# Smaller closing steps, earlier addresses and an earlier check in a graph layer with a mixture of experts

## The chip, the cores and the metric

The kernel runs on one core of one Trainium2 chip. The metric is the time of one execution in microseconds (us) on the device. A core has five engines, each with its own program that it works through in order: TensorE (PE in the profile, its weight loads PEld), VectorE (DVE), ScalarE (ACT), GpSimd (POOL) and SyncE (SP). SyncE only issues transfers here; ScalarE and GpSimd issue some too. "SPq" and "ACTq" are these engines' instruction queues.

## The reference

6250 nodes with 256 features go through a graph layer and then through a mixture of 8 experts, each node to the two experts with the highest scores.

```python
deg = jnp.maximum(jax.ops.segment_sum(jnp.ones(dst.shape), dst, num_segments=6250), 1.0)
x = x + gnn(_layernorm(x), deg ** -0.5, W, b, src, dst)   # 106250 edges: (h @ W.T + b) * norm, summed by dst, * norm
h = _layernorm(x)
gate_scores = h @ Wg.T + bg                               # (6250, 8)
topk_scores, topk_idx = jax.lax.top_k(gate_scores, 2)
topk_probs = jax.nn.softmax(topk_scores)
for e in range(8):
    y = jax.nn.relu(h @ W1[e].T + b1[e]) @ W2[e].T + b2[e]   # 256 -> 1024 -> 256
    out = out + combine[:, e:e + 1] * y                     # combine holds the two probabilities
return x + out
```

All of it is float32.

## The kernel before

**Stream.** The nodes form 49 tiles of 128. The edges, sorted by destination, form 831 chunks of 128. A planner written in Python places the work in *slots*: slot s (L961 to L979) issues one indirect gather of 128 source rows on GpSimd (`gather`, L459), a mask on VectorE, the matmul that adds up chunk s on TensorE (`add_up`, L470), the *tasks* that are due in that slot, and as many pieces of expert work as a *credit* allows (`next_piece`, L938). The credit gains 1025 ns less the known work in each slot; `PIECES` (L57) says what a piece costs. Before slot 140, credit that is left is spent on filling matmuls (L978). As soon as all edges of a tile have been added up, its nodes go through normalisation, scores, choice of experts and sorting in stages of fixed slots, and are sent to queues in DRAM, one for each expert (`send`, L714).

**Steps.** Expert work goes in 61 steps: 52 with a slot of their own (`STREAM`, L38) and nine behind the stream (`TAIL`, L45). `choose` (L728) takes, on VectorE, the expert with most rows waiting, and up to n of its rows, n being the size of the step; it also notes in `at`, for every node, where its result will stand. SyncE loads the weights w1 (L775, 1028 KB) and w2 (L788, 1152 KB) and the rows (`xT`, L783). `up` (L808) has 8 pieces of four matmuls, each followed by a ReLU on ScalarE into `hid`. `down` (L820) has four pieces of four matmuls for each half of 128 rows; a slot behind the fourth, `leave` (L834) adds the bias on VectorE (y, L838) and SyncE writes y to `fyq` (L840). There are two output tiles `py`, so a half can start when the y of the half before last is done. From L928 to L936: up pieces of one step and down pieces of the step before it take turns.

**Behind the stream** (L997 to L1027) each slot s issues due tasks, at most one choice, one load of w2 and one of w1 and rows, one piece, and work of *reading back*: `DONE` (L71) lists after which step how many tiles are finished. When a listed step has been done for six slots and nothing is queued, `results` (L902) makes the addresses `rowat` of its tiles on VectorE; then GpSimd gathers the two results of each tile, one a slot (`read_back`, L907, three slots in four), into one of 12 buffers `yb`; eight slots later, or when more than ten wait, `take` (L988) adds them to the node rows on VectorE (`add_in`, L917). Every fourth tile a store of four tiles goes out from GpSimd (L994, L924).

**The end.** When the last gather of tiles 44 to 47 has been added, L1031 to L1051 make the addresses of tile 48, check that no row came later than its tile's bound (ten operations on VectorE and a matmul with one column, whose result `g.bad` decides at L1506 whether a slow second path runs), gather tile 48, and store the rest.

The order on each engine is the order in which this Python code issues (`manual_schedule`); waits are put in where data or buffers demand them.

Of the kernel before, what the change touches and what calls it, by code (L numbers as in the profile page):

```python
# [7 lines left out]
F32 = mybir.dt.float32  # L8
# [11 lines left out]
P = 128  # L20
N = 6250
NT = 49
# [22 lines left out]
TAIL = (256, 256, 256, 256, 256, 256, 128, 128, 128)  # L45
ROWS_OF = [n for s, n in STREAM] + list(TAIL)
USUAL = len(ROWS_OF)
START = [P + sum(ROWS_OF[:step]) for step in range(USUAL + 1)]

# [7 lines left out]
PIECES = {FT: (915, 870), P: (600, 870)}  # L57
# [91 lines left out]
def in_order(ctx: ExitStack, tc: tile.TileContext, g: Shared):  # L149
# [670 lines left out]
    def down(step, i, s):  # L820
        f = steps[step]
        a = i // 4
        if i % 4 == 0:
            f["py"] = psp.tile([P, D], F32, name="py")
        for b in (2 * (i % 4), 2 * (i % 4) + 1):
            nc.tensor.matmul(f["py"], f["hid"][:, b, a * P:(a + 1) * P], f["w2"][:, b * D:(b + 1) * D],  # L826
                             start=(b == 0), stop=(b == HB - 1))
        if i % 4 == 3:
            plan_at(s + 1, leave, step, a, f["py"], f["w2"])
        if i == 4 * ROWS_OF[step] // P - 1:  # L830
            del steps[step]


    def leave(step, a, py, w2):  # L834

        nonlocal gone
        y = work.tile([P, D], F32, name="y", bufs=4)
        nc.vector.tensor_add(y, py, w2[:, HB * D:])  # L838
        r0 = START[step] + a * P
        w = nc.sync.dma_start(yq[r0:r0 + P, :], y)  # L840
        free_order(w, reads, "results are written once, and read once written")
        writes.append((step, w))
        if a == ROWS_OF[step] // P - 1:
            gone += 1


# [91 lines left out]
    def next_piece(s):  # L938

        nonlocal curu, curd, done, upped, was  # L940
        was = next_kind(s)
        if was == "up":
            up(upped, curu)
            curu += 1
            if curu == HB:
                upped, curu = upped + 1, 0
        if was == "down":
            down(done, curd, s)
            curd += 1
            if curd == 4 * ROWS_OF[done] // P:  # L950
                done, curd = done + 1, 0
        return was

    with tc.manual_schedule():
        with rowp as rowpool:
# [5 lines left out]
            for s in range(NC):  # L961
# [8 lines left out]
                while credit > 0:  # L970
                    of = upped, done
                    kind = next_piece(s)
                    if not kind:
                        break
                    credit -= PIECES[ROWS_OF[of[kind == "down"]]][kind == "down"]
# [4 lines left out]
        with tc.tile_pool(name="ftail", bufs=2) as pool:  # L980
# [3 lines left out]
            got = asked = allowed = stored = 0  # L984
            latest = 0
            since = {}

            def take():  # L988
# [4 lines left out]
                if got == 2 * stored + 11:  # L993
                    store(stored, stored + 4, nc.gpsimd)  # L994
                    stored += 4

            while done < USUAL or tasks or len(plan) > 1 or asked < 2 * allowed or pend:  # L997
                for fn, args in tasks.pop(s, []):
                    fn(*args)
                if s > all_sent and s > max(STREAM)[0] + 6:  # L1000
                    if chosen < min(USUAL, upped + 4):
                        run(choose(chosen))
                        chosen += 1
                    if loaded2 < min(loaded1, gone + 3):
# [10 lines left out]
                if len(plan) > 1 and done > plan[0][0] and s >= since.get(plan[0][0], 0) + 6 \  # L1015
                        and asked == 2 * allowed:
                    step, t1 = plan.pop(0)
                    results(allowed, t1, float(START[step + 1]))
                    allowed = t1
                    latest = step  # L1020
                if asked < 2 * allowed and s % (4 if s > all_sent else 2):
                    pend.append((s, read_back(pool, rowat, asked // 2, asked % 2, latest)))
                    asked += 1
# [4 lines left out]

            results(allowed, NT, float(START[USUAL]))  # L1031
            late = work.tile([P, NT, 2], F32, name="late", bufs=1)
            missed = work.tile([P, 2], F32, name="missed")
            nc.vector.tensor_tensor(late, at, bounds, op=OP.is_ge)
            nc.vector.tensor_reduce(missed[:, 0:1], late, op=OP.add, axis=mybir.AxisListType.XY)
            nc.vector.tensor_reduce(missed[:, 1:2], most, op=OP.max, axis=mybir.AxisListType.X)
            nc.vector.tensor_scalar(missed[:, 1:2], missed[:, 1:2], float(SLOTS), None, op0=OP.is_gt)
            nc.vector.tensor_add(missed[:, 0:1], missed[:, 0:1], missed[:, 1:2])
            nc.vector.tensor_add(missed[:, 0:1], missed[:, 0:1], g.outside)
            ones = work.tile([P, 1], F32, name="ones")  # L1040
            nc.vector.memset(ones, 1.0)
            pm = psp.tile([1, 1], F32, name="pt", bufs=1)
            nc.tensor.matmul(pm, missed[:, 0:1], ones, start=True, stop=True)
            nc.vector.tensor_scalar(g.bad, pm, 1.0, None, op0=OP.min)
# [506 lines left out]
```

## Time and profile before

| | us |
|---|---|
| median of 9 runs | 1305.92 (1304.93 to 1308.49) |
| the profiled execution | 1304.85 |
| its span, first to last instruction | 1303.1 |
| gathers of edges on GpSimd, first and last start | 70.7, 1114.8 |
| TensorE's longest late gap, before step 52's first piece | 6.57, to 1169.22 |
| last down piece of step 60 ends on TensorE | 1281.08 |
| last addition ends on VectorE | 1296.34 |
| TensorE, VectorE, ScalarE, GpSimd busy | 1173.7, 979.5, 405.1, 907.9 |

The page gives busy shares, 40 slices of the span with the busy share of each engine in tenths, the chain of work that ended last, and groups of instructions. A timeline row reads: start, duration, engine, line, operation, tiles, count, and in brackets how long the engine had been idle before it and what ended that. In groups of matmuls the durations overlap, so starts are what counts.

### The profile page before, as it was taken

What the parts mean: (1) busy time and instruction counts of PE and PEld (TensorE: products, weight loads), DVE (VectorE), ACT (ScalarE), POOL (GpSimd) and SP (SyncE); (2) the same over time, 40 slices, a digit from 0 to 9 for tenths busy, and PEclk for the clock granted to TensorE, in tenths of its full rate; (3) what the DMA queues carried; (4) which work ended last, traced back from release to release, by engine and by line L of the source; (5) the groups of instructions that cost most, each with busy time, mean ns of one, the idle gap of its engine ahead of it and who ended that gap; (6) DMA issues with size and microseconds to landing.
All of it is one profiled execution on the core that took longest, in us unless ns stands there. A gap on an engine that the chain in (4) does not pass through costs nothing.

```text
span 1303.1 us, 24787 instructions
## 1 busy us (share of the span) xinstructions
PE 1173.7 (90%) x6562; PEld 914.1 (70%) x6562; DVE 979.5 (75%) x5472; ACT 405.1 (31%) x949; POOL 907.9 (70%) x976
## 2 busy tenths in 40 slices
PE   5368789799999899999999889899999999979993
PEld 5336567377777677777777667677777777758882
DVE  8924686767888878888888788887977785895532
ACT  3713233133333233333333233323232333222220
POOL 2167777777777777777777777777777777557733
PEclk9999989899999999999999999999999999989997
DMA  7463597878787887888888787878888887889983
GB/s 250 156 195 106 173 319 206 278 217 292 250 267 258 260 294 254 267 292 258 266 263 277 245 267 232 282 236 309 275 291 275 289 290 255 284 293 406 332 298 100
DMA packets 160927, 337.38 MB, mean 259 GB/s; under 512 B 26900, under 2 KB 106344, under 8 KB 145160
## 3 DMA queue, kind: packets, MB, share of 16 engines
q1 hardware_dynamic: 114348, 207.57, 45.6%
q0 software_dynamic: 46176, 127.59, 32.5%
q8 instruction: 54, 0.88, 0.3%
q14 instruction: 97, 0.79, 0.2%
q10 hardware_dynamic: 252, 0.53, 0.1%
HBM read 280.44 MB, written 55.16 MB: 258 GB/s over the span
## 4 chain that ended last, share of the span: by engine, by line
PE 59%; DMA 22%; DVE 10%; issue 3%; POOL 3%; ACT 1%; SPq 1%; POOLq 0%; ACTq 0%; DVEq 0%
PE ph L816 22%; PE py L826 19%; DMA rows<-ftable,src 16%; PE ps L475 10%; DMA yb<-fyq,rowat 3%; PE pt L568 3%; PE ps L978 2%; POOL yb L909 1%; PE px L700 1%; DMA xT<-fhq 1%; POOL rows L461 1%; PE ph L518 1%; ACT hf L364 1%; DMA fhq<-ordered 1%; PE count L295 1%
## 5 line engine op out<-in xcount | busy, mean ns | idle before, releaser
L461 POOL DMA_INDIRECT rows<-ftable,src x831 | 792.2, 953 | 274.7 <-issue 103.3
L816 PE MATMUL ph<-xT,w 128*128 128x256 f32 (+1 forms) x1952 | 474.8, 370 | 10.9 <-DMA xT<-fhq 8.3
L826 PE MATMUL py<-w,hid 128*128 128x256 f32 x1760 | 450.5, 381 | 0.1
L816 PEld LDWEIGHTS ph<-xT,w 128*128 128x128 f32 x1952 | 351.4, 191 | 115.5 <-issue 27.8
L818 ACT ACTIVATE hid<-ph,w 128x256 f32<-128x256 f32 (+1 forms) x488 | 220.3, 452 | 576.6 <-PE ph L816 468.7
L826 PEld LDWEIGHTS py<-w,hid 128*128 128x128 f32 x1760 | 329.3, 190 | 73.8 <-issue 3.4
L475 PE MATMUL ps<-rows,mask 128*128 128x512 f16 x831 | 312.4, 382 | 63.0 <-DMA rows<-ftable,src 33.3
L468 DVE TENSOR_SCALAR mask<-col_b,rel 128x128 f16<-128x128 bf16 x831 | 202.4, 270 | 8.5 <-PE ps L475 6.4
L909 POOL DMA_INDIRECT yb<-fyq,rowat x98 | 94.9, 969 | 62.6 <-issue 20.1
L475 PEld LDWEIGHTS <-mask 128*128 128x128 f16 x831 | 82.2, 100 | 56.0 <-issue 21.7
L575 DVE SCALAR_TENSOR_TENSOR xr<-pt,norm,xr 128x256 f32<-128x256 f32 x49 | 23.7, 484 | 92.5 <-PE pt L568 92.4
L838 DVE TENSOR_TENSOR y<-py,w 128x256 f32<-128x256 f32 x110 | 46.1, 419 | 62.4 <-PE py L826 62.1
L535 DVE SCALAR_TENSOR_TENSOR rolled<-rolled,keep,ps 128x256 f32<-128x256 f32 x149 | 70.5, 473 | 23.2 <-PE ps L475 23.2
L550 ACT ACTIVATE whole<-rolled 32x256 f32<-32x256 f32 (+2 forms) x156 | 63.8, 409 | 59.7 <-DVE rolled L538 57.4
L917 DVE SCALAR_TENSOR_TENSOR xr<-yb,prob,xr 128x256 f32<-128x256 f32 x98 | 46.1, 481 | 36.9 <-DMA yb<-fyq,rowat 36.2
L538 DVE TENSOR_TENSOR rolled<-ps,rolled 128x256 f32<-128x256 f32 x150 | 63.6, 424 | 5.1
L568 PE MATMUL pt<-gw,uT 128*128 128x264 f32 x196 | 51.9, 387 | 0.0
L639 ACT ACTIVATE h2s<-h 128x256 f16<-128x256 f32 x49 | 20.3, 414 | 91.8 <-DVE h L630 91.7
L978 PE MATMUL ps<-nothing 128*128 128x512 f16 x162 | 48.1, 415 | 0.0
L568 PEld LDWEIGHTS pt<-gw,uT 128*128 128x128 f32 x196 | 37.4, 191 | 12.7 <-issue 2.0
L295 PE MATMUL count<-oh,ol 128*16 128x8 bf16 (+2 forms) x898 | 28.8, 175 | 15.6 <-DVE oh L281 13.3
L597 DVE TENSOR_SCALAR rs<-ry,rv 128x1 f32<-128x1 f32 x147 | 39.7, 270 | 1.9
(187 smaller groups left out, 1133.5 us busy)
## 6 DMA issues: line engine op xcount, KB each, us to landing
w<-in_W SPq DMA_DIRECT2D x61, 1152.0 KB
w<-in_W SPq DMA_DIRECT2D x61, 1028.0 KB
fhq<-ordered SPq DMA_DIRECT2D x392, 64.0 KB
fyq<-y SPq DMA_DIRECT2D x110, 128.0 KB
rows<-ftable,src POOLq DMA_INDIRECT x831
xT<-fhq SPq DMA_DIRECT2D x49, 256.0 KB
out<-xr POOLq DMA_DIRECT2D x11, 512.0 KB
xr<-in_x SPq DMA_DIRECT2D x6, 896.0 KB
```

The source lines that it names most:

```text
L461: nc.gpsimd.indirect_dma_start(out=rows[c], out_offset=None, in_=table[:, :], in_offset=bass.IndirectOffsetOnAxis(ap=g.src[:, c:c + 1], ax ...
L468: nc.vector.tensor_scalar(masks[c], g.col_b[:, r:r + P], g.rel[:, c:c + 1], None, op0=OP.is_equal)
L475: nc.tensor.matmul(sums[w], masks.pop(c), rows.pop(c), start=(c == chunks[0]), stop=(c == chunks[-1]))
L535: nc.vector.scalar_tensor_tensor(new, rolled, keeps[kept[w]], ps[:, 0:D], op0=OP.mult, op1=OP.add)
L538: nc.vector.tensor_add(new, ps[:, D:2 * D], new)
L550: nc.scalar.activation(whole[t][p0:p1, :], new[p0:p1, :], AF.Copy)
L568: nc.tensor.matmul(pl, uT[:, k, :], gw[:, k, :], start=(k == 0), stop=(k == 1))
L816: nc.tensor.matmul(ph[:, :n], w1[:, k * H + b * P:k * H + (b + 1) * P], f["xT"][:, :n, k], start=(k == 0), stop=(k == 1))
L818: nc.scalar.activation(f["hid"][:, b, :n], ph[:, :n], AF.Relu, bias=w1[:, 2 * H + b:2 * H + b + 1])
L826: nc.tensor.matmul(f["py"], f["hid"][:, b, a * P:(a + 1) * P], f["w2"][:, b * D:(b + 1) * D], start=(b == 0), stop=(b == HB - 1))
L909: r = nc.gpsimd.indirect_dma_start(out=yb, out_offset=None, in_=yq[0:START[upto + 1], :], in_offset=bass.IndirectOffsetOnAxis(ap=where[:, ...
L978: nc.tensor.matmul(sums[WINDOW[s]], nothing[:, 0:P], nothing, start=False, stop=False)
```

## The change

The steps behind the stream get smaller, from 1920 rows in all to 1632, and need no longer be multiples of 128; `down` and `leave` work on what rows there are (m). In the planner an up piece costs `29 * rows // 8` ns, at least 300. When all steps have been issued, addresses are made in the next slot, whatever is still queued, and a gather goes out in every slot; tile 48 goes through the same loop, and stores issued then leave from ScalarE and SyncE. The check becomes a task in parts (`verdict`) that starts four slots behind the choice of the last step.

```diff
-TAIL = (256, 256, 256, 256, 256, 256, 128, 128, 128)
+TAIL = (256, 256, 224, 208, 192, 176, 128, 128, 64)
+HALVES = [-(-n // P) for n in ROWS_OF]
-PIECES = {FT: (915, 870), P: (600, 870)}
+DOWN = 870
...
+        m = min(P, ROWS_OF[step] - a * P)
         for b in (2 * (i % 4), 2 * (i % 4) + 1):
-            nc.tensor.matmul(f["py"], f["hid"][:, b, a * P:(a + 1) * P], f["w2"][:, b * D:(b + 1) * D],
+            nc.tensor.matmul(f["py"][:m], f["hid"][:, b, a * P:a * P + m], f["w2"][:, b * D:(b + 1) * D],
...
-        nc.vector.tensor_add(y, py, w2[:, HB * D:])
+        m = min(P, ROWS_OF[step] - a * P)
+        nc.vector.tensor_add(y[:m], py[:m], w2[:m, HB * D:])
-        w = nc.sync.dma_start(yq[r0:r0 + P, :], y)
+        w = nc.sync.dma_start(yq[r0:r0 + m, :], y[:m])
...
+    def verdict():
+        late = work.tile([P, NT, 2], F32, name="late", bufs=1)
+        missed = work.tile([P, 2], F32, name="missed")
+        nc.vector.tensor_tensor(late, at, bounds, op=OP.is_ge)
+        nc.vector.tensor_reduce(missed[:, 0:1], late, op=OP.add, axis=mybir.AxisListType.XY)
+        yield
+        nc.vector.tensor_reduce(missed[:, 1:2], most, op=OP.max, axis=mybir.AxisListType.X)
+        nc.vector.tensor_scalar(missed[:, 1:2], missed[:, 1:2], float(SLOTS), None, op0=OP.is_gt)
+        yield
+        nc.vector.tensor_add(missed[:, 0:1], missed[:, 0:1], missed[:, 1:2])
+        nc.vector.tensor_add(missed[:, 0:1], missed[:, 0:1], g.outside)
+        ones = work.tile([P, 1], F32, name="ones")
+        nc.vector.memset(ones, 1.0)
+        yield
+        yield
+        pm = psp.tile([1, 1], F32, name="pt", bufs=1)
+        nc.tensor.matmul(pm, missed[:, 0:1], ones, start=True, stop=True)
+        yield
+        yield
+        nc.vector.tensor_scalar(g.bad, pm, 1.0, None, op0=OP.min)
...
-                    credit -= PIECES[ROWS_OF[of[kind == "down"]]][kind == "down"]
+                    credit -= DOWN if kind == "down" else max(300, 29 * ROWS_OF[of[0]] // 8)
...
                 if got == 2 * stored + 11:
-                    store(stored, stored + 4, nc.gpsimd)
+                    store(stored, stored + 4, nc.scalar if gone == USUAL else nc.gpsimd)
                     stored += 4
+                elif got == 2 * NT - 2:
+                    store(stored, NT - 1, nc.sync)
+                elif got == 2 * NT:
+                    store(NT - 1, NT)
...
                         chosen += 1
+                        if chosen == USUAL:
+                            in_parts(s + 4, verdict)
...
-                if len(plan) > 1 and done > plan[0][0] and s >= since.get(plan[0][0], 0) + 6 \
-                        and asked == 2 * allowed:
+                if plan and done > plan[0][0] and (done == USUAL or s >= since.get(plan[0][0], 0) + 6 and not queue):
                     step, t1 = plan.pop(0)
                     results(allowed, t1, float(START[step + 1]))
+                    queue += [(t, j, step) for t in range(allowed, t1) for j in range(2)]
                     allowed = t1
-                if asked < 2 * allowed and s % (4 if s > all_sent else 2):
-                    pend.append((s, read_back(pool, rowat, asked // 2, asked % 2, latest)))
-                    asked += 1
+                if queue and (done == USUAL or s % (4 if s > all_sent else 2)):
+                    t, j, step = queue.pop(0)
+                    pend.append((s, read_back(pool, rowat, t, j, step)))
...
-            results(allowed, NT, float(START[USUAL]))
...
-            last = [read_back(pool, rowat, t, j) for t in range(allowed, NT) for j in range(2)]
-            if stored < allowed:
-                store(stored, allowed, nc.sync)
-            for t, j, yb in last:
-                add_in(t, j, yb)
-                if j:
-                    store(t, t + 1, nc.sync if t % 2 else nc.scalar)
```

More of the change, by code (lines that the diff above doesn't have):

```diff
@@ L829, in down @@
             plan_at(s + 1, leave, step, a, f["py"], f["w2"])
-        if i == 4 * ROWS_OF[step] // P - 1:
+        if i == 4 * HALVES[step] - 1:
             del steps[step]
@@ L837, in leave @@
         y = work.tile([P, D], F32, name="y", bufs=4)
-        nc.vector.tensor_add(y, py, w2[:, HB * D:])
+        m = min(P, ROWS_OF[step] - a * P)
+        nc.vector.tensor_add(y[:m], py[:m], w2[:m, HB * D:])
         r0 = START[step] + a * P
-        w = nc.sync.dma_start(yq[r0:r0 + P, :], y)
+        w = nc.sync.dma_start(yq[r0:r0 + m, :], y[:m])
         free_order(w, reads, "results are written once, and read once written")
         writes.append((step, w))
-        if a == ROWS_OF[step] // P - 1:
+        if a == HALVES[step] - 1:
             gone += 1
+    def verdict():
[18 more added lines that the diff above has]
+        nc.vector.tensor_scalar(g.bad, pm, 1.0, None, op0=OP.min)
     tasks = {}
@@ L949, in next_piece @@
             curd += 1
-            if curd == 4 * ROWS_OF[done] // P:
+            if curd == 4 * HALVES[done]:
                 done, curd = done + 1, 0
@@ L983, in in_order @@
             plan = list(DONE)
-            got = asked = allowed = stored = 0
-            latest = 0
+            got = allowed = stored = 0
+            queue = []
             since = {}
@@ L993, in take @@
                 if got == 2 * stored + 11:
-                    store(stored, stored + 4, nc.gpsimd)
+                    store(stored, stored + 4, nc.scalar if gone == USUAL else nc.gpsimd)
                     stored += 4
-            while done < USUAL or tasks or len(plan) > 1 or asked < 2 * allowed or pend:
+                elif got == 2 * NT - 2:
+                    store(stored, NT - 1, nc.sync)
+                elif got == 2 * NT:
+                    store(NT - 1, NT)
+            while done < USUAL or tasks or plan or queue or pend:
                 for fn, args in tasks.pop(s, []):
@@ L1014, in in_order @@
                     since[over] = s
-                if len(plan) > 1 and done > plan[0][0] and s >= since.get(plan[0][0], 0) + 6 \
-                        and asked == 2 * allowed:
+                if plan and done > plan[0][0] and (done == USUAL or s >= since.get(plan[0][0], 0) + 6 and not queue):
                     step, t1 = plan.pop(0)
                     results(allowed, t1, float(START[step + 1]))
+                    queue += [(t, j, step) for t in range(allowed, t1) for j in range(2)]
                     allowed = t1
-                    latest = step
-                if asked < 2 * allowed and s % (4 if s > all_sent else 2):
-                    pend.append((s, read_back(pool, rowat, asked // 2, asked % 2, latest)))
-                    asked += 1
+                if queue and (done == USUAL or s % (4 if s > all_sent else 2)):
+                    t, j, step = queue.pop(0)
+                    pend.append((s, read_back(pool, rowat, t, j, step)))
                 if pend and (gone == USUAL or len(pend) > 10 or s >= pend[0][0] + 8):
@@ L1027, in in_order @@
                 s += 1
-            results(allowed, NT, float(START[USUAL]))
[L1032 to L1044, printed above, removed]
-            last = [read_back(pool, rowat, t, j) for t in range(allowed, NT) for j in range(2)]
-            if stored < allowed:
-                store(stored, allowed, nc.sync)
-            for t, j, yb in last:
-                add_in(t, j, yb)
-                if j:
-                    store(t, t + 1, nc.sync if t % 2 else nc.scalar)
 @with_exitstack
```

## The prediction

> **What bounds the kernel now.** I read the page first (shares, slices), then the chain of waits, then the timelines of the last 140 us, one engine at a time. The rows that set the pace:
>
> ```profile
> span 1303.1 us, 24787 instructions
> ...
> POOL 2167777777777777777777777777777777557733
> ...
> L461 POOL DMA_INDIRECT rows<-ftable,src x831 | 792.2, 953 | 274.7 <-issue 103.3
> ```
>
> GpSimd stands at 7 tenths in every slice of the stream: a gather takes 0.95 us and 0.30 us lie ahead of it, so 831 of them need 831 x 1.25 = 1039 us, and the first and last start at 70.7 and 1114.8. The stream goes at GpSimd's pace, and the change touches none of its gathers. What can move lies behind 1115 us. The chain of waits there:
>
> ```profile
> 1241.06 0.06 DVE xr L917
> ...
> 1244.22 6.35 DMA yb<-fyq,rowat
> 1250.66 0.09 DVE xr L917
> 1250.75 0.32 issue
> 1251.06 0.43 DVE y L838
> 1251.54 1.13 PE py L826 x4
> ```
>
> TensorE is busy without a gap from 1169 to 1281, but this piece of the chain shows that it is about to lose its lead. Its next output tile waits for VectorE's y; that y stands in VectorE's program behind additions (L917) whose rows GpSimd is still fetching. The y of 1251.06 belongs to a half that TensorE finished at 1243.4 (1242.41 + 1.02), 7.6 us before. So in this stretch three engines run level, and GpSimd has no idle but its 0.30 us from 1217 to 1250. The end, on GpSimd:
>
> ```profile
> 1267.75 0.97 POOL L909 DMA_INDIRECT yb<-fyq,rowat  x1 [15.51 <-DVE rowat L904]
> 1277.75 0.94 POOL L909 DMA_INDIRECT yb<-fyq,rowat  x1 [4.01 <-DMA fyq<-y]
> 1282.74 0.95 POOL L909 DMA_INDIRECT yb<-fyq,rowat  x1 [0.30 <-issue]
> 1283.68 0.81 POOL L924 DMA_DIRECT2D out<-xr  x1
> 1284.79 0.97 POOL L909 DMA_INDIRECT yb<-fyq,rowat  x1 [0.30 <-issue]
> 1291.04 0.94 POOL L909 DMA_INDIRECT yb<-fyq,rowat  x1 [2.77 <-DVE late L1034]
> 1292.29 0.94 POOL L909 DMA_INDIRECT yb<-fyq,rowat  x1 [0.30 <-issue]
> ```
>
> GpSimd has run dry by 1252 and idles 15.5 us for step 57. Ten gathers follow the y of step 59 (1274.85 to 1275.27): eight from 1277.75, with a store between them, then 2.77 us in which the addresses of tile 48 are missing, then the last two. Their additions end at 1296.34; 6.8 us of store, branch and end follow, which the change leaves as they are.
>
> **Part 1, the close.** From the end of y 59 to the last addition: 1296.34 - 1275.27 = 21.1 us. After the change the addresses of tile 48 are made as soon as the last pieces are issued, and the store is ScalarE's. The terms: 2.5 us to the first gather (1275.27 to 1277.75), nine times 1.25, and from the start of a last gather to the end of its addition 3.4 (1287.32 to 1290.69): 17.1 us. **Gain 4.0**; by parts, 0.8 for the store (1282.74 to 1284.79 instead of 1.25), 2.5 for the wait (2.77 - 0.30), 0.7 for a last gather that meets no store. If it meets the store of tiles 44 to 47, which SyncE now issues behind their last addition, it takes 4.0 (1292.29 to 1296.34), and the gain is 3.3. The y of step 60 must be written before tile 48 is read: five up pieces and four down ones behind y 59, 2.7 + 3.5, then 2.5 for y and write, 8.7 us against the 12.5 at which its gather starts, so it is covered. ScalarE's new store (0.52 as at L926) stands behind its last hid and ahead of the final store, ten microseconds early: nothing.
>
> The Trainium skill, in Trainium Kernel Development and Optimization, Key Constraints, says that DMAs of SyncE, ScalarE and GpSimd share the same 16 engines, so that spreading them saves only issue time; by it the moved store is worth its 0.8 us and no more, which is how it is priced above.
>
> **Part 2, fewer rows.** Tail steps of 256 cost 0.905 us for an up piece and 0.865 for a down one (1248.57, 1249.48, 1250.34); an up piece of 128 costs 0.455 (1252.50 to 1252.96). That is 3.5 ns per row and piece, 28 ns per row and step. Steps 54 to 57 lose 32, 48, 64, 80 rows: 0.9 + 1.35 + 1.8 + 2.25 = 6.3 us. Their down pieces stream the same 256 columns of w2 and still come in two halves: no gain. Step 60 has three up pieces between down ones, 0.23 less each (0.7); its other five run alone, where four weight loads take 0.53 already, as
>
> ```profile
> 1276.90 0.53 PEld L816 LDWEIGHTS ph<-xT,w 128*128 128x128 f32 x4 [0.20 <-ACT hid L818]
> ```
>
> shows: 0 to 0.2. So TensorE has **7.0 us less work**. Weights are the same bytes and SyncE issues them in the same order. That the sizes suffice I worked out from the inputs: routing every node by the reference and taking the largest queue each time, the nine steps find 199, 186, 183, 172, 154, 139, 128, 89 and 1 rows, and no row comes later than its tile's bound.
>
> But the y of step 56's first half still comes when GpSimd and VectorE get there, about 1250. TensorE would only wait there: of the 6.3 us most is not collected.
>
> **Part 3, the check.** Its ten vector operations (1290.68 to 1291.87, 1.2 us) go behind the choice of step 60, and its matmul into TensorE's program ahead of the fifth down piece of step 56. In order, it holds what stands behind it until VectorE has done the products: four down pieces of step 56, the up pieces of 57, then the y of 56 and 57, SyncE's writes of them, the loads of w2 59 and w1 60 in SyncE's queue behind those (w1 60 issued at 1258.59, used after 1269.8: 11 us of cover), and the close. VectorE's program has them behind the second addition of tile 38, which in the profile of before is the third of these three:
>
> ```profile
> 1245.83 1.39 DVE L917 SCALAR_TENSOR_TENSOR xr<-yb,prob,xr 128x256 f32<-128x256 f32 x3
> 1247.14 0.15 DVE L904 SCALAR_TENSOR_TENSOR rowat<-at 128x2 int32<-128x2 f32 x1
> ```
>
> 1247.1 + 1.2 = 1248.3, and 1248.4 on TensorE, which passed this place at 1244.18 before and would be there about 1239 now (1244.18 less 0.9, 1.35, 1.8 and half of 2.25). **A new wait**, and step 56 goes on 4.2 us later than before. From there to step 57's first down piece: four down at 0.865, four up of 176 rows at 0.62, 5.9 us instead of 7.4 (1244.18 to 1251.54): 2.8 us late. Then the clock:
>
> ```profile
> 1169.22 2.04 PE L816 MATMUL ph<-xT,w 128*128 128x256 f32 x4 [6.57 <-DMA xT<-fhq]
> 1171.07 1.61 PE L826 MATMUL py<-w,hid 128*128 128x256 f32 x4
> 1172.51 1.07 PE L816 MATMUL ph<-xT,w 128*128 128x256 f32 x4
> ```
>
> After 6.57 idle us the granted clock was 0.54 for 3.3 us, and two pieces took 1.85 and 1.44 instead of 0.905 and 0.865: 1.5 us. After 2.01 idle at 1134.58 it was 0.62; after 1.38 at 1152.12 it stayed 1.00. I take 1.5 (bounds 0 and 1.5): 4.3 late at step 57. Less 0.7 in step 60's pieces, y 59 ends **3.6 us later**, at 1278.9.
>
> TensorE: Matmul & The Clock Gate, Part 1, of the Trainium skill has half the clock after an idle window of some 3.4 us and as long again to warm up; by it the loss would be 1.7 us, and the 2.01 us stall would have cost nothing, where this trace shows 0.62.
>
> How exact is 1248.3? *Earlier:* the last addition that kept VectorE waiting started at 1241.06 on a gather issued at 1236.54, 4.5 us; the gather of 1280.24 was added 2.75 us after issue (1282.99). By that, 1.8 earlier. *Later:* the gathers of tile 38 (up to 1241.72) could take the 7.94 us of the gather at 1201.97 if step 58's w2 falls on them: added from 1249.7, checked at 1251.3, 3.0 later. Also, the choice for step 58 (1211.20 to 1214.86) now precedes the addresses of tile 28, which GpSimd awaits at 1210.8: up to 3.2 more idle there, of which the 1.2 at 1215.67 comes back; 0 to 2.0, inside the 3.0.
>
> **Part 4, the rest.** Planner costs: 128-row up pieces count 464 instead of 600, so 18 more filling matmuls (L978, 162 now) fall into slots 117 to 121: 18 x 0.415 = 7.5 us at most, hidden because TensorE waits 11.2 us for gathered rows between 90 and 200; without that cover, up to 7.5. By the end of the stream it is one piece ahead (0.9 us), which ends in the 6.57 us wait for xT. Read-backs after the last step come each slot: GpSimd's 1.25 hides that.
>
> **Sum.** -4.0 + 3.6 = **-0.4 us**. Span and time of the profiled execution are 1303.1 and 1304.85; the median 1305.92 is 1.07 above it. 1304.85 - 0.4 + 1.07 = **1305.5**.
>
> **Rivals.** *The check does not bind* (VectorE has caught up, or its matmul finds the products ready). For: between 1252 and 1262 VectorE does wait for TensorE. Against: at 1251.06 it is 7.6 us behind. Then step 57 begins where y 56 allows, about 1250.2, 1.3 earlier than 1251.54; -1.3 - 0.7 - 4.0 = -6.0, 1299.9. With every row's gain, -7.0 - 4.0 = -11, 1294.9; against that speaks that GpSimd has nothing to give from 1217 to 1250.
>
> *The check comes late, and this decides:* VectorE reaches it 3.0 us later, by step 58's weights or the moved choice. Place: TensorE, fifth down piece of step 56. -0.4 + 3.0 = +2.6, and +3.3 if the last gather meets the store too: 1308.8. It is slower than before from a check done after 1248.7. For: such latencies stand in the rows. Against: most gathers of 1236 to 1242 land quickly.
>
> *It does not do what it says* (a row misses its step, the second path runs): the last step holds one row for 64 places; under 1 in 100.
>
> **How the numbers follow.** A measurement tells about 0.2%, 2.6 us, from no change. Check binds near 1248 (1303.3 to 1308.5): 0.55; check does not bind: 0.25; late: 0.20. The range: -0.4 - 1.8 - 1.5 = -3.7 below, +2.6 above, so 1302.2 to 1308.5; widened to 1301.5 for part of the first rival.
>
> **What would show it.** TensorE idle for over 4 us at a 1-column matmul about 1240 to 1248, with a granted clock near 0.5 behind it; an earlier gap of a few us at a py; y 59 near 1279; then ten gathers 1.25 apart. Wrong, if TensorE has no gap there, or y 59 ends before 1275.

## The result and the profile after

On one chip the changed kernel took **1310.71 us** (median of 11 runs, 1309.01 to 1316.55) and the kernel before 1306.23 (34 runs): ratio **1.0041**, 95% interval 1.0031 to 1.0050, so 5.4 us slower by the ratio (the two medians are 4.5 us apart). The forecast was 1305.5, with 1301.5 to 1308.5 as its range. The profiled execution took 1312.97 us with a span of 1311.1, 2.3 us above its median, while the one of before lay 1.4 under its own; so differences between the two profiles are somewhat larger than those between the medians.

The page of the changed kernel, its span and GpSimd's edge gathers:

```profile
span 1311.1 us, 24818 instructions
...
L462 POOL DMA_INDIRECT rows<-ftable,src x831 | 792.0, 953 | 275.0 <-issue 97.5
```

The stream is what it was (274.7 us of idle before, 275.0 now; last gather at 1114.87 instead of 1114.80), and step 52's first piece starts at 1169.33 instead of 1169.22. All of the difference lies behind it. TensorE's timeline there (start, duration, engine, line, operation, tiles, count, and in brackets the idle time ahead of it and what ended it):

```profile
1237.64 1.13 PE L828 MATMUL py<-w,hid 128*128 128x256 f32 x4 [3.03 <-DVE y L841]
...
1252.46 0.19 PE L867 MATMUL pt<-ones,missed 128*1 128x1 f32 x2 [8.61 <-DVE ones L863]
1252.58 1.97 PE L828 MATMUL py<-w,hid 128*64 128x256 f32 x4
...
1267.18 1.06 PE L828 MATMUL py<-w,hid 128*48 128x256 f32 x4
1268.18 0.72 PE L817 MATMUL ph<-xT,w 128*128 128x128 f32 x4
1268.83 1.06 PE L828 MATMUL py<-w,hid 128*48 128x256 f32 x4
```

Three things are new. TensorE waits 3.03 us for a y. It waits 8.61 us at the check's matmul, the place that the prediction named. And behind it the pieces are slow, first while the clock is low, and later, at a full clock, where a half has 48 rows: down piece plus up piece take 1.65 us (1267.18 to 1268.83) where they took 1.32 with 128 rows (1252.96 to 1254.28 before). The windows view gives the clock (stretch and its length, then the busy times of TensorE, its weight loads, VectorE, ScalarE and GpSimd, the granted clock, the DMA share and GB/s):

```profile
1244.00:1252.40 8.40, 0.00 (x0) 0.00 (x0) 5.60 (x32) 0.30 (x1) 6.71 (x7) 0.66 0.98 352
1252.40:1258.20 5.80, 5.74 (x18) 3.24 (x18) 3.12 (x9) 0.41 (x1) 1.75 (x2) 0.61 0.75 272
```

VectorE's timeline shows why the check is late: its operations stand between additions that wait for gathered rows.

```profile
1249.93 0.54 DVE L942 SCALAR_TENSOR_TENSOR xr<-yb,prob,xr 128x256 f32<-128x256 f32 x1 [1.83 <-DMA yb<-fyq,rowat]
1250.40 0.25 DVE L854 TENSOR_TENSOR late<-at,bounds 128x98 f32<-128x98 f32 x1
...
1252.35 0.06 DVE L863 MEMSET ones<- 128x1 f32 x1
```

And GpSimd's timeline, at one early place and at the close:

```profile
1214.95 0.94 POOL L934 DMA_INDIRECT yb<-fyq,rowat  x1 [4.01 <-DVE rowat L929]
...
1289.20 0.94 POOL L934 DMA_INDIRECT yb<-fyq,rowat  x1 [5.38 <-DMA fyq<-y]
...
1300.63 0.95 POOL L934 DMA_INDIRECT yb<-fyq,rowat  x1 [0.30 <-issue]
```

At 1214.95 GpSimd has waited 4.01 us for addresses that now stand behind the choice of step 58 in VectorE's program; before, two waits of 0.71 and 1.48 stood there:

```profile
1211.15 0.95 POOL L909 DMA_INDIRECT yb<-fyq,rowat  x1 [0.71 <-DVE rowat L904]
...
1215.67 0.94 POOL L909 DMA_INDIRECT yb<-fyq,rowat  x1 [1.48 <-DVE rowat L904]
```

At the close the ten gathers start 1.27 apart on average (1289.20 to 1300.63), without a store or a wait between them.

**Two lengths** serve for all runs below: from the start of step 52's first piece to the end of the y of step 59, and from there to the end of the last addition (the *close*). They leave out the stream, whose length differs from run to run. Each is read from one profiled execution, so a difference of a us or two between them needs the ratios beside it.

| | to y 59 | close | both |
|---|---|---|---|
| before | 106.05 | 21.07 | 127.12 |
| after | 117.39 | 17.48 | 134.87 |

The close gained 3.6 us. The part ahead of it lost 11.3.

### The profile page after: what moved, and what is told of

The parts are those of the page before. It is cut to its first block, busy times and chain, and to the rows that moved or that the text cites. A ratio compares the mean times of both kernels' runs of the same rounds, so it can differ in the third digit from the quotient of the medians.

```text
span 1311.1 us, 24818 instructions
## 1 busy us (share of the span) xinstructions
PE 1177.8 (90%) x6580; PEld 911.2 (69%) x6580; DVE 980.1 (75%) x5472; ACT 403.6 (31%) x949; POOL 906.7 (69%) x975
## 5 line engine op out<-in xcount | busy, mean ns | idle before, releaser
L462 POOL DMA_INDIRECT rows<-ftable,src x831 | 792.0, 953 | 275.0 <-issue 97.5
L817 PE MATMUL ph<-xT,w 128*128 128x256 f32 (+6 forms) x1952 | 473.6, 369 | 7.7 <-DMA xT<-fhq 7.6
L828 PE MATMUL py<-w,hid 128*128 128x256 f32 (+1 forms) x1760 | 453.3, 382 | 3.0 <-DVE y L841 3.0
L817 PEld LDWEIGHTS ph<-xT,w 128*128 128x128 f32 x1952 | 352.4, 192 | 114.3 <-issue 30.5
L819 ACT ACTIVATE hid<-ph,w 128x256 f32<-128x256 f32 (+6 forms) x488 | 218.8, 449 | 603.6 <-PE ph L817 478.5
L828 PEld LDWEIGHTS py<-w,hid 128*128 128x128 f32 (+1 forms) x1760 | 324.2, 188 | 77.1 <-issue 4.9
L841 DVE TENSOR_TENSOR y<-py,w 128x256 f32<-128x256 f32 (+4 forms) x110 | 46.2, 420 | 72.2 <-PE py L828 70.6
L1003 PE MATMUL ps<-nothing 128*128 128x512 f16 x180 | 52.3, 409 | 0.0
L1003 PEld LDWEIGHTS <-nothing 128*128 128x128 f16 x180 | 18.7, 105 | 32.4 <-issue 17.9
```

The source lines that it names most:

```text
L462: nc.gpsimd.indirect_dma_start(out=rows[c], out_offset=None, in_=table[:, :], in_offset=bass.IndirectOffsetOnAxis(ap=g.src[:, c:c + 1], ax ...
L817: nc.tensor.matmul(ph[:, :n], w1[:, k * H + b * P:k * H + (b + 1) * P], f["xT"][:, :n, k], start=(k == 0), stop=(k == 1))
L819: nc.scalar.activation(f["hid"][:, b, :n], ph[:, :n], AF.Relu, bias=w1[:, 2 * H + b:2 * H + b + 1])
L828: nc.tensor.matmul(f["py"][:m], f["hid"][:, b, a * P:a * P + m], f["w2"][:, b * D:(b + 1) * D], start=(b == 0), stop=(b == HB - 1))
L1003: nc.tensor.matmul(sums[WINDOW[s]], nothing[:, 0:P], nothing, start=False, stop=False)
```

## The experiments

Ratios are to the kernel before, in a series of alternate runs on the same chip, with 95% intervals. Some kernels were measured a second time, since the first series had another pace; those are told last. "Check late" is the changed kernel with the whole check begun when the last piece has been issued.

### One part at a time

Check late:

```diff
                         if chosen == USUAL:
-                            in_parts(s + 4, verdict)
...
                     since[over] = s
+                    if done == USUAL:
+                        in_parts(s + 2, verdict)
```

> The changed kernel with the check begun once the last piece is issued, everything else as changed. Theory 1 (the check's matmul in TensorE's order is the loss): the 8.6 us gap at the one-column matmul goes, TensorE next waits for the y of step 56's first half, which VectorE reaches some 1.5 us sooner without the check's operations; step 57's first down piece starts at 1252 to 1254 instead of 1261.8, y 59 ends at 1277 to 1279 instead of 1286.7, and the time is 1301 to 1303.5 us, against 1310.7. Rival (GpSimd's chain of gathers is late by 2.15 us and VectorE waits for it in any case, so the check's matmul only stands where a wait for the y would stand): y 59 ends after 1283 and the time stays above 1307.

Old steps, check early:

```diff
-TAIL = (256, 256, 224, 208, 192, 176, 128, 128, 64)
+TAIL = (256, 256, 256, 256, 256, 256, 128, 128, 128)
```

> The changed kernel with the old steps (six of 256 rows, three of 128); check, close and order as changed. Theory 3 (second halves of 64 and 48 rows make TensorE slower than full ones, and fewer rows only lengthen the wait at the check): TensorE comes to the check some 5 us later, waits 3 to 4 us there instead of 8.6, and y 59 ends at 1284 to 1285 instead of 1286.7; the time is 1308 to 1309.5. Rival (fewer rows are a gain, if a small one): 1311 to 1314. Under both, the pieces behind the check that work on 128 columns take 0.865 (down) and 0.455 (up of 128 rows) once the clock is full.

Both edits, so that the close alone is left:

> The new close alone: old steps, check begun once the last piece is issued. If the close is worth what was forecast (3.3 to 4.0 us) and nothing else in it costs: y 59 ends where it does in the kernel before, at 1275 to 1276, the last addition ends 17.1 to 17.8 us later, and the time is 1302 to 1303 us, against 1306.2 before. Rival (read-backs and stores of the new close get in the way of others): above 1304.

Addresses first: the block that pops `plan` and makes the addresses stands ahead of the choice in the slot (for steps before the last), instead of behind it.

> The changed kernel with the addresses of finished tiles made ahead of a choice that falls in the same slot; nothing else. Theory 2 (the choice of step 58 ahead of the addresses costs GpSimd 2.15 us, and the check's products come late by that): the gap of GpSimd at 1214.95 falls from 4.0 to about 1.6 us, the matmul of the check starts about 2 us sooner (1250.3 instead of 1252.5), and the time is 1308 to 1309. Rival (the lateness has another source, the additions' own latencies): the check starts at 1252 and the time stays at 1310 to 1311.5.

| | ratio | check's matmul, from step 52 | to y 59 | close |
|---|---|---|---|---|
| changed kernel | 1.0041 (1.0031 to 1.0050) | 83.13 | 117.39 | 17.48 |
| check late | 0.9985 (0.9969 to 1.0001) | | 107.69 | 18.57 |
| old steps, check early | 1.0029 (1.0014 to 1.0045) | 82.41 | 115.27 | 17.53 |
| old steps, check late | 0.9972 (0.9957 to 0.9987) | | 106.02 | 18.63 |
| addresses first | 1.0017 (1.0003 to 1.0030) | 78.86 | 112.52 | 17.41 |

The four corners give each part's price twice. **The early check**: 1.0041 - 0.9985 = 0.0056 with the new steps, 1.0029 - 0.9972 = 0.0057 with the old ones, 7.3 and 7.4 us of 1306. **The new steps**: 1.0041 - 1.0029 = 0.0012 and 0.9985 - 0.9972 = 0.0013, 1.6 to 1.7 us. That is no gain; that it is a loss is not shown by the times, since each ratio is known to about 0.0015 and the two late-check medians, of one series, are 0.1 us apart (1307.32 and 1307.23). **The close**: 0.9972, a gain of 3.7 us (1.7 to 5.6); y 59 stands where it stood before (106.02 against 106.05). Along one path over the corners 7.4 + 1.6 - 3.7 = 5.3, which must come out near the 5.4; what is tested is that each part costs the same beside either form of the other.

Not all went as expected. The two absolute times forecast for a late check were missed (1307.3 for 1301 to 1303.5, and 1307.2 for 1302 to 1303) since that chip ran the kernel before in 1310.2; by ratio the close alone was as expected, and the check late came out some 2 us worse than hoped, though in its profile step 57's first down piece (1252.69) and y 59 (1277.69) stand where the theory had them. The old steps gained 1.6 us on the changed kernel where 1.2 to 2.7 was expected, and the wait at the check was 6.5 instead of 3 to 4, as TensorE came to it only 1.4 us later than with the new steps, not 5. With a late check the close is 1.1 us longer: in both runs the last gather's data comes 2.2 us after VectorE is ready for it, against 1.1 in the changed kernel. The store of tiles 44 to 47 goes out 0.8 to 0.9 us behind the start of that gather in all three, so it does not tell them apart. Something else does: in all seven runs with a late check one transfer of 16 KB on queue q8, which the profile calls "instruction", starts 1.2 to 1.8 us behind the start of the last gather and takes 1.0 to 1.6 us, and the last addition begins 3.8 to 4.4 us behind that start; in the twelve other runs with the new close no such transfer falls there, and it begins after 3.0 to 3.1. That the transfer holds up the gather is likely, but not tested.

Addresses first brought the check forward and 3.1 us of time. GpSimd's timeline, then the check on TensorE, in that run:

```profile
1213.51 0.95 POOL L934 DMA_INDIRECT yb<-fyq,rowat  x1 [0.30 <-DVE li L737]
...
1217.50 0.95 POOL L934 DMA_INDIRECT yb<-fyq,rowat  x1 [0.95 <-DVE rowat L929]
```

```profile
1251.49 0.19 PE L867 MATMUL pt<-ones,missed 128*1 128x1 f32 x2 [7.07 <-DVE ones L863]
```

The 4 us gap is gone, and the matmul stands 78.86 us behind step 52's first piece (1251.49 - 1172.63) instead of 82.4 to 83.3 in the three runs that have the gap and the early check.

### Matmul or vector operations

The check's vector operations stay, and its matmul moves:

```diff
         yield
         yield
+        for _ in range(20):
+            yield
         pm = psp.tile([1, 1], F32, name="pt", bufs=1)
```

> The check's vector operations in their place, its matmul 20 slots later in TensorE's order; on a chip where the kernel before takes 1306 to 1310 us. If the wait in TensorE's order is the loss: no gap at a one-column matmul, from step 52's first piece to the y of step 59 107 to 108.5 us (117.39 in the changed kernel, 107.69 with the whole check late), the close 17.5 us, ratio 0.997 to 0.9985. If the check's vector operations delay the y's in VectorE's order by themselves: 109 us or more, and 0.9995 or more. On the other chip, where the check hardly waits, both this and the changed kernel stand at 0.9966.

Ratio **0.9982** (0.9970 to 0.9993), 108.95 to y 59, close 17.37. TensorE's timeline:

```profile
1242.24 1.13 PE L828 MATMUL py<-w,hid 128*128 128x256 f32 x4 [3.68 <-DVE y L841]
...
1257.08 1.13 PE L828 MATMUL py<-w,hid 128*128 128x256 f32 x4 [1.32 <-DVE y L841]
```

So the place of one matmul with one column in TensorE's program is worth 1.0041 - 0.9982 = 0.0059, 7.7 us, which is all of the check's price: with its vector operations left where they were, nothing of it remains that the ratio can tell. The length to y 59 lies a little above the band given (108.5), since the two waits for a y, 3.68 and 1.32, remain.

### Halves of few rows

No second half under 80 rows, first with the check late, then early:

```diff
-TAIL = (256, 256, 224, 208, 192, 176, 128, 128, 64)
+TAIL = (256, 256, 224, 208, 208, 208, 128, 128, 128)
```

> No second half under 80 rows, check late, once more for the same reason. Theory 3: 106 to 107 us from step 52's first piece to the y of step 59 (107.69 with halves of 64 and 48 rows), ratio 0.9970 to 0.9980; rival: 109 us, above 0.9990.

> The changed kernel, check early, no half under 80 rows; on a chip where the kernel before takes 1306 to 1310 us. Small halves cost where TensorE sets the pace: from the check's matmul to the end of the y of step 59 32.2 us (34.26 in the changed kernel), ratio 1.002 to 1.0035 (the changed kernel 1.0031 to 1.0050). Rival (the loss comes back from another wait): 34 us or more, ratio as the changed kernel's.

| | ratio | to y 59 | close |
|---|---|---|---|
| check late | 0.9989 (0.9974 to 1.0004) | 110.18 | 18.00 |
| check early | 1.0025 (1.0012 to 1.0039) | 115.30 | 17.23 |

With the check late the theory failed: no gain on the 0.9985 with small halves, and the rival's length. The pieces were faster, but TensorE only came sooner to a y that was not there: it waited 2.37 us at one half and 3.52 at another, the second with a slow clock behind it. (The profiled execution was 5 us above its kernel's median; step 52 begins 4 to 5 us later in it than in the other runs of the series, so this length leaves most of that out.) With the check early, where TensorE sets the pace from the check to the end, it held. TensorE's timeline of that run:

```profile
1254.24 0.19 PE L867 MATMUL pt<-ones,missed 128*1 128x1 f32 x2 [6.02 <-DVE ones L863]
...
1267.88 1.02 PE L828 MATMUL py<-w,hid 128*80 128x256 f32 x4
1268.74 0.62 PE L817 MATMUL ph<-xT,w 128*128 128x128 f32 x4
1269.19 1.02 PE L828 MATMUL py<-w,hid 128*80 128x256 f32 x4
```

A pair takes 1.31 us with 80 rows and 1.65 with 48, and from the check to y 59 it is 31.99 us (32.2 expected) instead of 34.26. The time moves from 1.0041 to 1.0025, 2.1 us, though 112 more rows are worked on; the two intervals overlap, so it is the profile's length that shows it.

Is it the size or the change of size? In the next run the four down pieces of such a half follow each other instead of alternating with up pieces:

```diff
         if first and second:
+            if curd >= 4 and ROWS_OF[done] - P <= P // 2:
+                return "down"
             return "down" if was == "up" else "up"
```

> As the run with the check late, with the changed steps, but the four down pieces of a half of 64 or 48 rows are issued one behind the other instead of between up pieces. If the cost lies in changing between 128 columns and fewer: the second to fourth of them take 0.86 to 0.92 us instead of 1.01, the pairs lose most of their 0.34 us, and from step 52's first piece to the y of step 59 it is 105.5 to 106.5 us. If fewer columns are slower in themselves: still 1.0 us a piece, and 107 to 108 us.

This run is of a series of another pace (below), so its lengths say little, but at a full clock the pieces can be read. TensorE's timeline, step 57:

```profile
1510.73 4.61 PE L828 MATMUL py<-w,hid 128*128 128x256 f32 x20
1515.27 3.08 PE L817 MATMUL ph<-xT,w 128*128 128x128 f32 x20
```

The first group is one piece of 128 rows and four of 48. Five pieces of 128 would take 5 x 0.863 = 4.31 us, these took 4.54 (1510.73 to 1515.27), 0.23 more; and the first up piece behind them is 0.1 longer than at full halves (3.08 for the group of five, 2.98 in the changed kernel at 1278.49). Together 0.33 us, once, where alternating pays 0.33 at each of four pairs. The single matmuls of the trace say where it lies: those on 48 columns start 0.216 us apart, like those on 128; only the first and second of them, and the first two of the up piece behind, are late, by 0.09, 0.04, 0.09 and 0.11. The last half of the program, alone in a row, agrees; before it has 128 rows, in the changed kernel 64:

```profile
1277.46 3.62 PE L826 MATMUL py<-w,hid 128*128 128x256 f32 x16
```

```profile
1288.71 3.67 PE L828 MATMUL py<-w,hid 128*64 128x256 f32 x16
```

So the first answer holds: all of the cost is in the change from 128 columns to 64 or fewer and back, 0.33 us for both, and nothing in the small piece itself.

### Whose pace keeps the rows from being collected

Check late and addresses first:

> Check late and addresses ahead of a choice in the same slot, once more for the same reason. Theory 2: TensorE's wait for a y at 1237 under 1.5 us and the clock full behind it, 105 to 106 us from step 52's first piece to the y of step 59; rival: 107 to 108 us.

Ratio 0.9983 (0.9969 to 0.9997), 107.88 to y 59, close 18.14. The waits on TensorE:

```profile
1235.47 1.13 PE L828 MATMUL py<-w,hid 128*128 128x256 f32 x4 [1.26 <-DVE y L841]
...
1251.31 1.55 PE L828 MATMUL py<-w,hid 128*128 128x256 f32 x4 [2.33 <-DVE y L841]
```

The rival was right: the first wait shrank from 3.6 to 1.26, and 2.33 us came at the next y. So moving the addresses pays only while the early check waits for VectorE.

If GpSimd's chain is the pace, it must be made shorter. In the next two runs the stores of the tail go out from ScalarE, 14 slots behind the last addition, so that ScalarE does not wait for it; addresses come first, and the check begins behind step 57. The two differ in the steps alone: the old ones, and those without small halves.

```diff
-                    store(stored, stored + 4, nc.scalar if gone == USUAL else nc.gpsimd)
+                    if done < USUAL - 2:
+                        plan_at(s + 14, store, stored, stored + 4)
+                    else:
+                        store(stored, stored + 4, nc.scalar if gone == USUAL else nc.gpsimd)
...
                     since[over] = s
+                    if done == USUAL - 3:
+                        in_parts(s + 2, verdict)
```

> The version with ScalarE's stores, with the old steps of 256 and 128 rows. If fewer rows are collected once GpSimd's chain is shorter: with the old steps TensorE has no wait behind step 52, needs its 105 to 106 us from step 52's first piece to the y of step 59, and the ratio to before is 0.9965 to 0.998, so that the same version with fewer rows is 2 to 4 us faster. Rival (the gain of that version is not in the rows): the two within 1 us of each other.

> The version with ScalarE's stores once more, since the run before it fell on a chip whose TensorE clock was held at about 0.93 and whose 35 runs of the kernel before took 1558 us. On a chip where that kernel takes 1306 to 1310: from step 52's first piece to the y of step 59 102 to 104 us, ratio 0.993 to 0.9955, by the theory that GpSimd's chain keeps the rows from being collected; by its rival 105.5 us or more and 0.9965 or more.

| | ratio | to y 59 | close |
|---|---|---|---|
| old steps | 0.9971 (0.9958 to 0.9984) | 106.23 | 17.39 |
| 256 to 208, then 128 | **0.9951** (0.9936 to 0.9967) | 103.76 | 17.46 |

As the theory had it: the same cut of rows that gained nothing with the check late gains 0.0020 here, 2.6 us, and TensorE's longest wait behind step 52 is 0.61 us. The two runs are of one series, and their difference is known to within 1.7 us. Between the run without small halves and the check late and this one lie three edits, though: the stores, the addresses first and the check behind step 57. Addresses first gave nothing by themselves (above, with small halves); that it is the stores alone was not tested. With the old steps the three give nothing more than the close, since TensorE never waited. The second of these beats both kernels: 1301.68 us against 1307.99 for the kernel before in that series.

### In two series in which TensorE is late

Eight runs belong to two series in which the kernel before took 1558 and 1577 us, with a mean granted clock of 0.92 to 0.93 in the profiles: four with the check late or, with ScalarE's stores, behind step 57, and four with it early. The expectations call this another chip, whose clock was held at about 0.93. Neither is shown. The chips have the numbers 4 and 3 in these two series, and number 4 stands beside the series between them too, in which the kernel before took 1307.99 us. And the clock of these traces is full or half at any time, as elsewhere; it is half for 204 to 260 us in all instead of 54 to 86, and TensorE has more waits.

> As the run with the check late, with the steps 256, 256, 224, 208, 208, 208, 128, 128, 128: no second half is under 80 rows, and 112 more rows are worked on. Measured from the first piece of step 52 to the end of the y of step 59 (106.05 us before, 117.39 in the changed kernel, 107.69 with the check late). Theory 3 (a half of 64 or 48 rows costs about 0.34 us more per pair of pieces than one of 80 or more, eight pairs, 2.7 us): down pieces of 80 columns at 0.865, and 106 to 107 us although the added rows cost 1.4; the ratio to before 0.9970 to 0.9980. Rival (no such cost; the slow pairs come from the clock or from what ScalarE does): 109 us, and a ratio above 0.9990.

> As the run with the check late, and the addresses ahead of a choice in the same slot. Theory 2 (the choice ahead of the addresses costs GpSimd some 2 us, and this is the 3.0 to 3.6 us wait of TensorE for a y at 1237 and the slow clock behind it): that wait is under 1.5 us, the clock stays full behind it, and from step 52's first piece to the y of step 59 it is 105 to 106 us instead of 107.7. Rival (the wait only moves to the next y, since GpSimd's chain sets the pace): 107 to 108 us.

> A version that should beat both: steps 256, 256, 224, 208, 208, 208, 128, 128, 128; addresses ahead of a choice in the same slot; the check issued behind step 57 instead of behind the choice; the stores of finished tiles issued by ScalarE, 14 slots behind their last addition, instead of by GpSimd. If GpSimd's chain is what keeps fewer rows from being collected: eight stores of 0.8 us leave it, TensorE waits nowhere over 1 us behind step 52, from step 52's first piece to the y of step 59 it is 102 to 104 us, and the ratio to before is 0.993 to 0.9955. Rival (the additions wait for the gathers' data and not for their issue, or ScalarE's stores hold up its hid): 105.5 us or more, and 0.9965 or more.

> The changed kernel, check early, with the steps 256, 256, 224, 208, 208, 208, 128, 128, 128 (no half under 80 rows). Small halves cost where TensorE sets the pace: from the check's matmul to the end of the y of step 59 32.2 us instead of 34.3 (2.7 less for the halves, 0.6 more for the added rows of steps 57 and 60), and 1 to 2 us less time than the changed kernel in g4. Rival (what is lost there comes back from another wait, as it did with the check late): 34 us or more, and no difference over 0.5 us.

The next one puts 18 matmuls of `nothing` into a spare tile ahead of the check's matmul (`nc.tensor.matmul(warm, nothing[:, 0:P], nothing, start=True, stop=True)`).

> The changed kernel with 18 matmuls on zeros in front of the check's matmul, which fill the wait (18 x 0.415 = 7.5 of 8.6 us). If the slow clock behind the wait is a cost of its own: the granted clock behind the check is full, step 57's first down piece starts 7.3 to 7.6 us behind the check's matmul instead of 9.24, and the time is 1.5 to 2 us under g4. If the slow pieces there are the halves of 64 rows alone: 9 us, and the time of g4.

> The changed kernel with the check's vector operations in their place and its matmul 20 slots later in TensorE's order. If the wait in TensorE's order is the loss: no gap at a one-column matmul, from step 52's first piece to the y of step 59 107 to 108.5 us as with the whole check late, the close 17.5 us, and a ratio to before of 0.997 to 0.9985. If the check's vector operations delay the y's in VectorE's order by themselves: 109 us or more, and 0.9995 or more.

> The changed kernel itself, as the measure for the three beside it: ratio to before 1.003 to 1.005; check's matmul 82 to 84 us behind step 52's first piece and the y of step 59 34 us behind that.

| | ratio |
|---|---|
| no small halves, check late | 0.9971 (0.9941 to 1.0002) |
| small halves together, check late | 0.9969 (0.9939 to 0.9999) |
| check late, addresses first | 0.9974 (0.9947 to 1.0002) |
| ScalarE's stores, fewer rows | **0.9930** (0.9901 to 0.9958) |
| no small halves, check early | 0.9956 (0.9925 to 0.9987) |
| wait filled | 0.9981 (0.9953 to 1.0008) |
| check's matmul 20 slots later | 0.9966 (0.9936 to 0.9996) |
| the changed kernel | 0.9966 (0.9938 to 0.9994) |

Here the changed kernel is the *faster* one, if barely by its interval. Its timeline on TensorE:

```profile
1501.24 1.65 PE L817 MATMUL ph<-xT,w 128*128 128x192 f32 x4 [5.77 <-issue]
...
1517.06 0.19 PE L867 MATMUL pt<-ones,missed 128*1 128x1 f32 x2 [0.74 <-DVE ones L863]
```

TensorE has stopped at up pieces for 6.6, 3.8 and 5.8 us in steps 53 and 56, by waits that the profile puts down to ScalarE's hid or to nothing, and comes to the check when VectorE has all but done it: 0.74 us of wait. That is the rival in which the check does not bind, in another setting, and moving the matmul then changes nothing (0.9966 twice). TensorE's waits being others here, the rows of this table are no test of the theories given with them. For the question whether the slow clock behind the wait is a cost of its own, the run with the filled wait says nothing here, as there was no wait to fill. Why TensorE stops at those up pieces is open; ahead of the hid that it waits for, ScalarE itself has stood 8.16, 6.70 and 8.14 us waiting for something that the profile calls "remote", a wait that ScalarE has nowhere in the changed kernel's first profile.

## Why the prediction was wrong

It named the place and the kind of the loss, gave the late check a chance of 0.20, and sized it wrongly. Its sum for y 59 can be set beside the profile, in us from step 52's first piece:

| step of the sum | forecast | measured |
|---|---|---|
| TensorE reaches the check (74.96 before) | -5.2 | -0.4 |
| it goes on from there | 79.2 | 83.13 |
| from there to y 59 (31.09 before) | 30.5 | 34.26 |
| y 59 against before | +3.6 | +11.3 |

**Part 1, the close: right.** 17.48 us in the profile against 17.1 to 17.8. The last gather meets the store of tiles 44 to 47 (0.87 us behind its start) and takes 3.6 us to the end of its addition, between the 3.4 and 4.0 given. Alone, with the check late, the close gains 3.7 us by the ratio, but 2.4 by its profile (21.07 - 18.63), for the 1.1 us told above.

**Part 3, when the check is done: the step that failed first.** The prediction took 1248.3 from the place that the check's operations have among VectorE's additions in the profile of before, and counted the moved choice of step 58 as "0 to 2.0, inside the 3.0". The three runs with the moved choice and the early matmul have the check at 82.4 to 83.3, the one without it at 78.9. So the moved choice is worth some 4 us at the check, twice the bound given. That 78.9 lies so near the forecast's 79.2 is partly luck: there the check's operations begin at 76.0 instead of 77.9, and take 2.8 us instead of 1.2, as an addition that waits for rows stands between their parts. In the changed kernel they begin at 81.1 and take 2.0. The beginning is 3.2 us late: GpSimd's chain is late by 2.15 (tile 38's second gather at 1243.87 instead of 1241.72), the rest is in when the gathered rows came; and 0.8 is in the operations, which the prediction priced as if they ran in one piece. (It also counts ten of them; the profile has seven ahead of the matmul and one behind.) That the wait is TensorE's alone, and not VectorE's load, the run with the moved matmul shows.

**Part 2, "No gain" for down pieces, with no loss weighed: the second.** Halves of 64 and 48 rows cost about 0.33 us a pair, eight pairs, 2.7 us; the run without them gives 2.3 us of it back in the profile and 2.1 in the time. The 0.7 us that step 60's short up pieces were to bring to y 59 is nothing: between down pieces a pair with 64 rows takes 1.31 us, like one with 128, and from the first down piece of step 59 to the start of its y it is 4.99 us instead of 5.02.

**The clock**: 1.5 us, its upper bound, was taken. In the changed kernel the four pairs behind the check take 9.24 us, where eight such pieces at a full clock take 7.3 (1258.26 to 1260.09, four times), so 1.9. With 2.7 for the halves, 0.7 for step 60 and 0.4 for the clock, the 3.8 us between 30.5 and 34.26 are accounted for.

**"Most is not collected": right, and for the reason given.** TensorE reached the check only 0.4 us sooner, after 3.03 us of waiting for a y; and with the three edits that relieve GpSimd's chain 2.6 us of the cut in rows were collected.

**The rivals.** "The check comes late" was the case that came, with its place; its price of 3.0 us was too low (3.9 us at the check, and 3.8 behind it that the sum did not hold). (Its 1308.8, with the store met, adds 3.3 to a 1305.5 that already holds the -0.4; from 1305.92 it is 1309.2.) "The check does not bind" came in the later series, where the changed kernel was 5.4 us faster (0.0034 of 1577, with an interval from 0.9 to 9.8); that this is close to the forecast -6.0 says little, as TensorE waited elsewhere. The claim that smaller steps suffice was borne out by the profile: the second path does not run.

## What to carry to other kernels

A tiny operation that is put into an engine's program waits for its inputs with everything behind it, so ask when its inputs are ready in the order that the *changed* program will have, and place its consumer where that time has certainly passed: here 20 slots were worth 7.7 us. A cut in work on the engine that seems busiest pays only as far as the engine beside it can follow; shorten both chains together, and test each alone. Before work is cut to odd sizes, read in the trace what a piece of that size costs beside its neighbours, and keep pieces of one size together.

## What the runs showed of the hardware

**Changing to a small stationary operand and back costs 0.33 us, not the small operand.** Down pieces on 48 or 64 columns of `hid` took 1.00 to 1.01 us between up pieces, on 80, 96 and 128 columns 0.86, and the up pieces beside the small ones were 0.2 us longer as well. In a row, matmuls on 48, 64 and 128 columns all start 0.216 us apart.

**The length of a wait does not settle the clock behind it; where it falls does.** Behind 3.68 us (check's matmul moved) and 3.03 us (changed kernel) the next pieces ran at full speed; behind 2.33 us (check late, addresses first) and 3.60 us (check late) they were slow. In every trace of this case the granted clock changes only at whole multiples of 3.413 us from its other changes. Cut into such windows, the traces tell the waits apart by the idle time that falls into one window. The window with most of the 3.03 us, and then the one with the 2.33 us and the window behind it (stretch and length, TensorE's busy time first):

```profile
1233.07:1236.49 3.42, 1.54 (x9) 1.01 (x6) 0.17 (x1) 0.84 (x2) 2.80 (x3) 1.00 1.02 404
```

```profile
1248.47:1251.89 3.42, 1.09 (x7) 0.76 (x6) 1.93 (x5) 0.41 (x1) 1.89 (x2) 1.00 0.97 353
1251.89:1255.30 3.41, 3.41 (x12) 2.84 (x11) 1.85 (x5) 0.37 (x1) 0.80 (x1) 0.50 0.66 228
```

The waits of 3.03, 3.68 and 2.37 us (the last without small halves, check late) left at most 1.9 us idle in any window, and the clock stayed full. Those of 2.33, 3.50, 3.52, 3.60 and 8.61 us left 2.2 or more in one, and in the next window it was half. Over all 20 traces, from 250 us on, a window at full clock with more than 2.03 us idle was always followed by half the clock and one with less than 1.69 never; between the two both occur. The Trainium skill, in TensorE: Matmul & The Clock Gate, Part 1, has a free-running window of about 3.4 us, which agrees with this spacing; it gives half the clock after an idle window, where these traces have it after a window with 2.2 us of idle already.

**The same change has another sign in another setting**: 1.0041 where TensorE leads, 0.9966 where it comes late.
